# Two chained layers (transform convolution, selective scan): a new plan for the scan layer, its moments in PSUM, and table loads on change of set

## The chip, the cores and the metric

One NeuronCore of a Trainium2 chip runs one program. The time is device microseconds from launch to end, median of three runs, and apart from these runs there is one profiled execution, whose trace is read here. The engines are TensorE (PE in the profile; PEld is its weight load), VectorE (DVE), ScalarE (ACT), GpSimd (POOL) and SyncE (SP), which only issues DMAs. Each engine executes its own instructions in order and waits on semaphores.

## The reference

Layer 0 takes x of shape (4, 192, 128, 128) through a group norm, a 1x1 convolution to 48 channels, a fractional and a real Fourier branch, and a 1x1 convolution back, and adds x. Layer 1, which the change touches and the diff's title calls layer 2, does this with the result:

```python
x = x + _L1_conv_ref(_gn(x), ...)
# inside, with L = h * w tokens of 192 channels:
seq = (seq - mu) * lax.rsqrt(var + LN_EPS) * ln_g + ln_b
xs, z = jnp.split(jnp.einsum('blc,ec->ble', seq, in_proj_w), 2, axis=-1)
u = jax.nn.silu(conv1d(xs, conv_w, 4 taps, depthwise) + conv_b)
dt, Bm, Cm = jnp.split(jnp.einsum('bld,kd->blk', u, x_proj_w), ...)
dt = jax.nn.softplus(jnp.einsum('blr,dr->bld', dt, dt_proj_w) + dt_proj_b)
A = -jnp.exp(A_log)
# per token: 384 inner channels x 16 states
h = h * exp(dt * A) + (dt * u) * B_t
y = sum_over_states(h * C_t)
y = (y + u * Dp) * jax.nn.silu(z)
out = jnp.einsum('bld,cd->blc', y, out_proj_w)
```

## The kernel before

Layer 0 (`layer0`) takes the first 1.4 ms and is not touched. Layer 1 (`layer1`) cuts each of the 4 images into 32 **chunks** of T = 512 tokens, 128 chunks in all. The 384 inner channels are three tiles j = 0, 1, 2 of 128 partitions, and the 16 states are taken in pairs (G = 2). One tile with one pair is a **position**: 3 x 8 = 24 positions a chunk, 0 to 23, each with two scans. Below, "12.1" is the second scan of position 12.

**A scan.** `scans` (L938) runs `tensor_tensor_scan` on DVE over 512 tokens: h = da * h + db. The decay da = exp(dt * A) comes from ACT (`decay`, L860). The input db = dt * u * B comes in one of three ways, by the position's letter in `KINDS`: **V**, DVE multiplies (`product`, L881) into a PSUM bank; **O**, POOL multiplies both states at once (`inputs`, L892) into SBUF, and then da goes to a PSUM bank instead (`decay_there`); **P**, ACT scales the transposed dt * u (`scale`, L909, tile dbT, four buffers) and PE turns it back into PSUM (`turned_back`, L924). The PSUM tiles of these operands are called op and have three buffers, so an operand of scan s+3 has to wait until scan s is over. The da tiles in SBUF have four buffers.

**After the scans.** SP stores the last column of h as the next chunk's start (carry, L949). POOL multiplies h by C (hc, L951, 1,024 elements). Three positions later PE adds up hc over the states (`sums`, L964). The tile h has three buffers: position k+3 can start to write only when POOL has read h of position k and the carry DMA of k has landed.

**Around the scans.** Everything else that a chunk needs is placed by hand in `PLAN`: (position, phase, step, arguments). Positions below 0 are before the chunk's own first scan, those above 23 after its last, and the loop runs the plans of neighbouring chunks laid over each other; so a step at -20 falls on position 4 of the chunk being scanned, one at 32 on position 8 of a later one. A position's phases are S (before all else), A (after the first turning back and `sums`), M (between its two scans) and L (after them). The steps are, in order: `load_x`, `to_tokens` (PE), `moments` (DVE: bn_stats, bn_aggr), `rstd` (ACT, by Ln and Exp), `shift` (DVE), `normed` (ACT), `to_channels` (PE), `channels` (ACT, then a DMA that copies rows 0 to 63 of s, shifted by two tokens, to rows 64 to 127), `conv` (PE), `silu` (ACT), `proj_z` (PE), `proj_x` (PE), `xd_out` (ACT, then a DMA of B and C), `proj_dt` (PE), `softplus` (ACT), `dt_u` (POOL), `turn_b` and `b_out`, `turned` (PE) and `scale`, `dtu_copy` (ACT), `evacuate` (ACT), `turn` (PE), `gate` (DVE), `project_out` (PE), `add_x` (DVE). They share five PSUM banks, handed out in the order of release (`psum`, `done`).

**Queues.** SP issues the DMAs in the order of the code: the carry of each position, `load_x`, the DMA behind `xd_out`, the one behind `channels`, the output, and from position 19 on, through position 2 of the next chunk, the next chunk's B and C, copied to all partitions (`load_bc`, b and c, 512 KB each).

**Tables.** ACT's Silu, Softplus, and Ln with Exp lie in different table sets. `log_exp` (L661) loads the set for Ln and Exp; after each call of `silu` and of `softplus` the code calls it. The load of the Silu or Softplus set is added by the compiler in front of the first such instruction.

Of the kernel before, what the change touches and what calls it, by code (L numbers as in the profile page):

```python
# [121 lines left out]
def layer0(tc, x, xmid, st2, w):  # L122
# [409 lines left out]

KINDS = ("VOPPVVPO", "VOVPOVPP", "VOVPVPPO")

PLAN = (
# [21 lines left out]
)  # L559


def layer1(tc, xmid, out, st2, w, n_tok=S * S):
# [9 lines left out]
    with ExitStack() as ctx:  # L572
# [55 lines left out]
        ln = const("ln")  # L628
        wz = cp.tile([128, 2, NJ, 128], F32, name="wz")
        nc.sync.dma_start(out=wz, in_=w["wi"][:, :, 1])  # L630
        wc = cp.tile([128, NJ, 6, 128], F32, name="wc")
        for half in range(2):
            nc.sync.dma_start(
# [23 lines left out]
        NGR = NJ * NG  # L657
        got = [{} for _ in range(total)]

        def log_exp():  # L660
            nc.scalar.preload_act_table_set("natural_log_exp_and_others")  # L661

        def load_x(i):
            b, ch = divmod(i, NCHUNK)
# [19 lines left out]
        def row(g, blk):  # L684
            return g["X", blk // 2][0][:, blk % 2 * C : (blk % 2 + 1) * C]

        def moments(i, half):
            g = got[i]
            if half == 0:
                g["mv"] = tp.tile([128, NBLK, 2], F32, name="mv")  # L690
            st = tp.tile([128, 2, 6], F32, name="st")
            for blk in range(2):
                nc.vector.bn_stats(st[:, blk, :], row(g, 2 * half + blk))
            for blk in range(2):
                nc.vector.bn_aggr(g["mv"][:, 2 * half + blk, :], st[:, blk, :])

        def rstd(i):
            g = got[i]
            rs = g["rs"] = tp.tile([128, NBLK], F32, name="rs")
            nc.scalar.activation(rs, g["mv"][:, :, 1], AF.Ln, bias=eps)  # L700
            nc.scalar.activation(rs, rs, AF.Exp, scale=-0.5)  # L701

        def shift(i):
            g = got[i]
            sh = g["sh"] = tp.tile([128, NBLK], F32, name="sh")
            nc.vector.scalar_tensor_tensor(sh, g["mv"][:, :, 0], -1.0, g["rs"], ALU.mult, ALU.mult)

        def normed(i, half):
            g = got[i]
# [46 lines left out]
        def proj_z(i, j):  # L756
            g = got[i]
            psum(g, "z", j)
            z = g["z", j][0]
            nc.tensor.matmul(z, wz[:, 0, j, :], g["s"][:, 0, 3:], start=True, stop=False)  # L760
            nc.tensor.matmul(z, wz[0:64, 1, j, :], g["s"][0:64, 1, 3:], start=False, stop=True)  # L761

        def silu(i, us, zs):
            g = got[i]
            for j in us:
                t = g["u", j] = jp.tile([128, T], F32, name="u", bufs=5)
                nc.scalar.activation(t, g["c", j][0], AF.Silu, bias=cb[:, j : j + 1])  # L767
                done(g, "c", j)
            for j in zs:
                t = g["zs", j] = jp.tile([128, T], F32, name="zs", bufs=5)  # L770
                nc.scalar.activation(t, g["z", j][0], AF.Silu)
                done(g, "z", j)
            log_exp()

        def proj_x(i):
            g = got[i]
# [79 lines left out]
        def decay(s, da):  # L856
            n, k, q = states[s]
            j, sg = divmod(k, NG)
            st = sg * G + q
            nc.scalar.activation(da, got[n]["dt", j], AF.Exp, scale=A[:, j, st : st + 1])  # L860
            das[s] = da

# [31 lines left out]
        def turned(n, j):  # L894

            g = got[n]
            psum(g, "tu", j)
            g["pairs", j] = KINDS[j].count("P")
            for blk in range(NBLK):
                at = slice(blk * 128, (blk + 1) * 128)  # L900
                nc.tensor.transpose(g["tu", j][0][:, at], g["dtu", j][:, at], ident)  # L901

        def scale(n, j, sg):

            g = got[n]
            for st in range(sg * G, (sg + 1) * G):
                t = g["dbT", j, st] = scp.tile([128, NBLK, 128], F32, name="dbT")
                for blk in range(NBLK):
                    nc.scalar.activation(  # L909
                        t[:, blk, :], g["tu", j][0][:, blk * 128 : (blk + 1) * 128], AF.Identity,  # L910
                        scale=g["bT"][:, blk, st : st + 1],
                    )
            g["pairs", j] -= 1
            if not g["pairs", j]:
                done(g, "tu", j)
# [92 lines left out]
        def add_x(n, t):  # L1008
# [11 lines left out]
        does = dict(  # L1020
            load_x=load_x, to_tokens=to_tokens, moments=moments, rstd=rstd, shift=shift,
            normed=normed, to_channels=to_channels, channels=channels, conv=conv, proj_z=proj_z,
            silu=silu, proj_x=proj_x, xd_out=xd_out, proj_dt=proj_dt, softplus=softplus, dt_u=dt_u,
            turn_b=turn_b, b_out=b_out, dtu_copy=dtu_copy, turned=turned, scale=scale,
            evacuate=evacuate, turn=turn, gate=gate, project_out=project_out, add_x=add_x,
        )
# [193 lines left out]
```

## Time and profile before

| what | us |
|---|---|
| median of 3 runs (lowest, highest) | 11,274.59 (11,271.61, 11,287.38) |
| the profiled execution | 11,264.48 |
| its span, first to last instruction | 11,262.4 |
| PE, DVE, ACT, POOL busy in it | 10,025.0, 10,180.0, 9,562.4, 9,530.1 |
| mean granted TensorE clock | 0.958 |

The costliest groups of layer 1 on each engine are the scans on DVE (L938, two lines of 5,483.3 and 1,880.2 us), hc on POOL (L951, 7,220.3 us), the decays on ACT (L860, 3,191.1 and 1,096.8 us) and the transposing sums on PE (L964, 3,278.8 us). Reading such a table one has to keep in mind that these shares are of the whole span, layer 0 among them, where POOL does little. The times of the steps in layer 1 are read from the timeline of single chunks.

### The profile page before, as it was taken

The numbers are of one execution on the slowest core, as the hardware profiler recorded it, in microseconds if no ns is written. First come the engines' busy times: TensorE is split into PE (matmuls) and PEld (weight loads), VectorE is DVE, ScalarE is ACT, GpSimd is POOL, SyncE is SP. The second block draws the span as 40 slices with busy tenths as digits, with TensorE's granted clock in tenths as the row PEclk, the third lists the DMA queues.
The fourth block names the chain that finished last, engine by engine and source line by source line (L and its number), as shares of the span: only waits on it lengthen the run. The fifth ranks groups of instructions, "written<-read, shape, count | busy, mean of one in ns | idle before, by whom it ended". The sixth has DMA issues, their size and how long they took to land. (4 is left out here: it accounts for less than half of the span.)

```text
span 11262.4 us, 172048 instructions
## 1 busy us (share of the span) xinstructions
PE 10025.0 (89%) x56050; PEld 6906.9 (61%) x56050; DVE 10180.0 (90%) x11329; ACT 9562.4 (85%) x20200; POOL 9530.1 (85%) x4342
## 2 busy tenths in 40 slices
PE   4777789999999999999999999999999999999998
PEld 2434366666666666666666666666666666666666
DVE  5566589999999999999999999999999999999999
ACT  2323199999999999999999999999999999999998
POOL 0000089999999999999999999999999999999999
PEclk8888699999999999999999999999999999999999
DMA  8786733333333333333333333333333333333333
GB/s 234 190 219 174 206 115 108 105 117 106 107 117 105 108 117 106 107 117 107 106 117 107 106 117 111 102 117 110 103 117 111 102 117 112 101 117 113 100 117 91
DMA packets 1330368, 1366.53 MB, mean 121 GB/s; under 512 B 918345, under 2 KB 969790, under 8 KB 1328830
## 3 DMA queue, kind: packets, MB, share of 16 engines
q1 hardware_dynamic: 1308990, 1292.60, 40.0%
q0 software_dynamic: 13312, 50.34, 1.4%
q10 hardware_dynamic: 7168, 12.59, 0.3%
q8 instruction: 446, 7.31, 0.3%
q14 instruction: 452, 3.70, 0.1%
HBM read 1179.79 MB, written 155.33 MB: 119 GB/s over the span
## 5 line engine op out<-in xcount | busy, mean ns | idle before, releaser
L951 POOL TENSOR_TENSOR hc<-h,c 128x1024 f32<-128x1024 f32 x3072 | 7220.3, 2377 | 400.6 <-DVE h L938 371.5
L938 DVE TENSOR_TENSOR_SCAN h<-da,carry,op 128x512 f32<-128x512 f32 x4464 | 5483.3, 1262 | 150.5 <-ACT xd L784 69.2
L964 PE MATMUL ps<-ident,hc 128*128 128x128 f32 x24576 | 3278.8, 278 | 10.8 <-POOL hc L951 10.8
L860 ACT ACTIVATE da<-dt,c_A_log 128x512 f32<-128x512 f32 x4608 | 3191.1, 748 | 97.3 <-DVE h L938 93.1
L964 PEld LDWEIGHTS ps<-ident,hc 128*128 128x128 f32 x24576 | 2892.2, 144 | 485.1 <-issue 458.5
L909 ACT ACTIVATE dbT<-ps,bT 128x128 f32<-128x128 f32 x9216 | 2475.7, 402 | 76.4 <-PE ps L901 65.3
L754 PE MATMUL ps<-s,wc 128*128 128x512 f32 x4608 | 2162.5, 596 | 23.7 <-DMA s<-s 7.6
L938 DVE TENSOR_TENSOR_SCAN h<-op,carry,db 128x512 f32<-128x512 f32 x1488 | 1880.2, 1270 | 174.4 <-POOL db L892 103.1
L924 PE MATMUL op<-ident,dbT 128*128 128x128 f32 x9216 | 1462.7, 285 | 589.9 <-DVE h L938 581.2
L892 POOL TENSOR_TENSOR db<-dtu,b 128x1024 f32<-128x1024 f32 x768 | 1843.9, 2401 | 5.0 <-DMA b<-dbc 5.0
L924 PEld LDWEIGHTS op<-ident,dbT 128*128 128x128 f32 x9216 | 1091.7, 145 | 1031.9 <-ACT rs L701 396.5
L881 DVE TENSOR_TENSOR op<-ps,b 128x512 f32<-128x512 f32 x2304 | 1548.5, 672 | 9.4 <-ACT ps L842 9.4
L860 ACT ACTIVATE op<-dt,c_A_log 128x512 f32<-128x512 f32 x1536 | 1096.8, 714 | 392.9 <-DVE h L938 392.7
L754 PEld LDWEIGHTS ps<-s,wc 128*128 128x128 f32 x4608 | 795.4, 190 | 673.2 <-issue 628.5
L1003 PE MATMUL ps<-yg,c_woT 128*96 128x512 f32 x1536 | 710.5, 598 | 7.6 <-ACT u L767 0.3
L661 ACT ACT_TABLE_LOAD x513 | 658.2, 1283 | 9.8 <-PEq L1210 0.7
L808 POOL TENSOR_TENSOR dtu<-dt,u 128x512 f32<-128x512 f32 x384 | 486.0, 1281 | 53.8 <-ACT dt L801 53.8
L495 POOL DMA_DIRECT2D xmid<-xt x64 | 41.3, 645 | 566.9 <-DVE xt L491 526.5
L1003 PEld LDWEIGHTS ps<-yg,c_woT 128*96 128x96 f32 x1536 | 233.1, 163 | 384.9 <-issue 273.0
L761 PE MATMUL ps<-s,wz 64*128 64x512 f32 x768 | 431.0, 641 | 0.0
L760 PE MATMUL ps<-s,wz 128*128 128x512 f32 x768 | 419.3, 628 | 0.7 <-DVE xm L1010 0.5
L979 PE MATMUL ps<-ddp,u 128*128 128x128 f32 x3072 | 418.0, 280 | 0.0
(165 smaller groups left out, 9376.4 us busy)
## 6 DMA issues: line engine op xcount, KB each, us to landing
c<-dbc SPq DMA_DIRECT2D x1024, 512.0 KB, 5.9
b<-dbc SPq DMA_DIRECT2D x768, 512.0 KB, 5.1
xt<-in_x SPq DMA_DIRECT2D x176, 768.0 KB, 7.8
xmid<-xt POOLq DMA_DIRECT2D x64, 768.0 KB, 5.6
xm<-xmid SPq DMA_DIRECT2D x128, 384.0 KB, 3.4
carry<-h SPq DMA_DIRECT2D x3072, 1.0 KB, 1.9
out<-xm SPq DMA_DIRECT2D x128, 384.0 KB, 3.1
s<-s SPq DMA_DIRECT2D x128, 128.5 KB, 3.8
```

Source lines behind the costliest of these rows:

```text
L661: nc.scalar.preload_act_table_set("natural_log_exp_and_others")
L754: nc.tensor.matmul(g["c", j][0], wc[:, j, k, :], rhs, start=k == 0, stop=k == 5)
L808: nc.gpsimd.tensor_tensor(g["dtu", j], g["dt", j], g["u", j], ALU.mult)
L860: nc.scalar.activation(da, got[n]["dt", j], AF.Exp, scale=A[:, j, st : st + 1])
L881: nc.vector.tensor_tensor(dbs[s], g["dp", j][0], g["b", k % NG][:, q, :], ALU.mult)
L892: nc.gpsimd.tensor_tensor(db, _bc(g["dtu", j], 1, G), g["b", sg], ALU.mult)
L909: nc.scalar.activation(t[:, blk, :], g["tu", j][0][:, blk * 128 : (blk + 1) * 128], AF.Identity, scale=g["bT"][:, blk, st : st + 1],)
L924: nc.tensor.transpose(db[:, blk * 128 : (blk + 1) * 128], t[:, blk, :], ident)
L938: nc.vector.tensor_tensor_scan(h[:, q, :], das.pop(s), dbs.pop(s) if db is None else db[:, q, :], 0.0 if ch == 0 else g["before"][:, j, st ...
L951: nc.gpsimd.tensor_tensor(hc, h, g["c", "b", sg], ALU.mult)
L964: nc.tensor.matmul(py[:, blk, :], hc[:, q, blk * 128 : (blk + 1) * 128], ident, start=first, stop=sg == NG - 1 and q == G - 1 and blk == N ...
L1003: nc.tensor.matmul(g["po", t][0][0:CH], woT[:, j, t * CH : (t + 1) * CH], g["yg", j], start=j == 0, stop=j == NJ - 1,)
```

## The change

Five things are done, all in layer 1.

1. `KINDS` swaps two letters in the rows of j = 0 and j = 2, with the same number of each letter in a row as before.
2. `PLAN` is new as a whole. `silu` is split into `silu_u` and `silu_z`, one tile a call, and `scale` takes one state instead of a pair, so that these can be placed singly.
3. The mean and variance that `bn_aggr` yields go to eight spare columns (384 to 391) of the PSUM bank that holds the second half of the tokens, instead of the SBUF tile mv; `rstd` and `shift` read them there.
4. The second matmul of `proj_z` has all 128 rows instead of 64; the weights of the added rows are set to zero once.
5. `log_exp` remembers the set that is loaded, and is called in front of each decay and `rstd` instead of after `silu` and `softplus`.

```diff
-KINDS = ("VOPPVVPO", "VOVPOVPP", "VOVPVPPO")
+KINDS = ("VOPPVVOP", "VOVPOVPP", "VOVPPVOP")
 PLAN = (
-    (-36, "A", "load_x"), (-34, "L", "to_tokens", 0), (-32, "S", "moments", 0),
-    (-32, "A", "to_tokens", 1), (-31, "S", "moments", 1), (-31, "A", "rstd"), (-30, "S", "shift"),
-    (-30, "M", "normed", 0), (-30, "M", "normed", 1), (-29, "S", "to_channels", 0),
-    (-29, "A", "channels", 0), (-28, "M", "to_channels", 1), (-28, "M", "channels", 1),
-    (-27, "S", "conv", 0, 0), (-27, "L", "conv", 1, 0), (-26, "L", "conv", 1, 1),
-    (-25, "M", "conv", 0, 1), (-24, "M", "conv", 1, 2), (-22, "L", "conv", 2, 0),
-    (-21, "M", "conv", 0, 2), (-21, "L", "silu", (0, 1), ()), (-17, "S", "conv", 2, 1),
-    (-16, "A", "conv", 2, 2), (-15, "L", "proj_z", 0), (-15, "L", "silu", (2,), (0,)),
-    (-13, "M", "proj_x"), (-11, "S", "xd_out"), (-11, "M", "proj_dt"), (-10, "M", "softplus"),
-    (-9, "M", "turn_b"), (-8, "A", "b_out"), (-7, "A", "dt_u", 0), (-7, "A", "dt_u", 1),
-    (-3, "L", "turned", 0), (-3, "L", "scale", 0, 2), (-2, "S", "dtu_copy", 0),
-    (1, "S", "dt_u", 2), (1, "A", "scale", 0, 3), (2, "S", "scale", 0, 6),
-    (4, "M", "dtu_copy", 1), (6, "S", "turned", 1), (6, "A", "scale", 1, 3),
-    (10, "S", "scale", 1, 6), (10, "A", "scale", 1, 7), (10, "M", "evacuate", 0),
-    (10, "M", "proj_z", 2), (11, "A", "proj_z", 1), (11, "M", "silu", (), (1, 2)),
-    (11, "L", "turn", 0), (12, "L", "dtu_copy", 2), (13, "M", "gate", 0), (16, "L", "turned", 2),
-    (17, "S", "scale", 2, 3), (17, "L", "scale", 2, 5), (19, "S", "scale", 2, 6),
-    (19, "M", "evacuate", 1), (21, "A", "turn", 1), (22, "S", "gate", 1),
-    (26, "L", "evacuate", 2), (29, "A", "turn", 2), (30, "A", "gate", 2),
-    (31, "A", "project_out", 0), (32, "L", "add_x", 0), (34, "S", "project_out", 1),
-    (35, "M", "add_x", 1),
+    (-35, "M", "load_x"), (-34, "M", "to_tokens", 1), (-34, "L", "to_tokens", 0),
+    (-33, "L", "moments", 0), (-32, "A", "moments", 1), (-31, "L", "rstd"), (-30, "M", "shift"),
+    (-30, "M", "normed", 0), (-30, "M", "normed", 1), (-30, "M", "to_channels", 1),
+    (-29, "L", "to_channels", 0), (-29, "L", "channels", 0), (-27, "L", "channels", 1),
+    (-26, "S", "conv", 0, 0), (-26, "L", "conv", 1, 0), (-25, "L", "conv", 1, 1),
+    (-24, "L", "conv", 1, 2), (-22, "S", "conv", 0, 1), (-20, "S", "silu_u", 1),
+    (-20, "S", "conv", 0, 2), (-20, "S", "silu_u", 0), (-20, "M", "conv", 2, 0),
+    (-19, "M", "conv", 2, 1), (-17, "A", "conv", 2, 2), (-16, "L", "silu_u", 2),
+    (-15, "L", "proj_z", 0), (-15, "L", "silu_z", 0), (-13, "S", "proj_x"), (-13, "M", "xd_out"),
+    (-11, "M", "proj_dt"), (-10, "S", "softplus"), (-9, "M", "dt_u", 1), (-8, "S", "turn_b"),
+    (-8, "M", "dt_u", 0), (-8, "M", "b_out"), (-4, "A", "turned", 0), (-2, "M", "scale", 0, 6),
+    (-2, "L", "dtu_copy", 0), (-1, "A", "scale", 0, 4), (0, "A", "scale", 0, 5),
+    (0, "M", "scale", 0, 15), (1, "S", "scale", 0, 7), (2, "M", "scale", 0, 14),
+    (4, "S", "turned", 1), (7, "A", "dt_u", 2), (7, "A", "dtu_copy", 1), (7, "A", "scale", 1, 6),
+    (7, "M", "scale", 1, 7), (9, "M", "scale", 1, 15), (10, "S", "proj_z", 1),
+    (10, "A", "scale", 1, 14), (10, "L", "scale", 1, 13), (10, "L", "scale", 1, 12),
+    (10, "L", "evacuate", 0), (11, "S", "proj_z", 2), (11, "M", "silu_z", 1),
+    (11, "M", "silu_z", 2), (11, "L", "turn", 0), (13, "S", "gate", 0), (13, "A", "dtu_copy", 2),
+    (17, "S", "turned", 2), (17, "S", "scale", 2, 6), (17, "M", "scale", 2, 7),
+    (18, "M", "scale", 2, 8), (18, "M", "scale", 2, 9), (18, "M", "evacuate", 1),
+    (19, "L", "scale", 2, 15), (20, "S", "scale", 2, 14), (21, "A", "turn", 1),
+    (22, "S", "gate", 1), (27, "A", "evacuate", 2), (29, "S", "turn", 2), (29, "M", "gate", 2),
+    (32, "S", "project_out", 0), (32, "L", "add_x", 0), (34, "S", "project_out", 1),
+    (34, "L", "add_x", 1),
 )
...
+        nc.vector.memset(wz[64:128, 1], 0.0)
...
         def log_exp():
-            nc.scalar.preload_act_table_set("natural_log_exp_and_others")
+            if table[0] != "log_exp":
+                nc.scalar.preload_act_table_set("natural_log_exp_and_others")
+                table[0] = "log_exp"
...
+        def mean_var(g):
+            return g["X", 1][0][:, 2 * C : 2 * C + 2 * NBLK].rearrange("p (k m) -> p k m", m=2)
...
-                nc.vector.bn_aggr(g["mv"][:, 2 * half + blk, :], st[:, blk, :])
+                nc.vector.bn_aggr(mean_var(g)[:, 2 * half + blk, :], st[:, blk, :])
...
-            nc.scalar.activation(rs, g["mv"][:, :, 1], AF.Ln, bias=eps)
+            log_exp()
+            nc.scalar.activation(rs, mean_var(g)[:, :, 1], AF.Ln, bias=eps)
...
-            nc.vector.scalar_tensor_tensor(sh, g["mv"][:, :, 0], -1.0, g["rs"], ALU.mult, ALU.mult)
+            nc.vector.scalar_tensor_tensor(
+                sh, mean_var(g)[:, :, 0], -1.0, g["rs"], ALU.mult, ALU.mult
+            )
...
-            nc.tensor.matmul(z, wz[0:64, 1, j, :], g["s"][0:64, 1, 3:], start=False, stop=True)
+            nc.tensor.matmul(z, wz[:, 1, j, :], g["s"][:, 1, 3:], start=False, stop=True)
...
-        def silu(i, us, zs):
-            g = got[i]
-            for j in us:
-                t = g["u", j] = jp.tile([128, T], F32, name="u", bufs=5)
-                nc.scalar.activation(t, g["c", j][0], AF.Silu, bias=cb[:, j : j + 1])
-                done(g, "c", j)
-            for j in zs:
-                t = g["zs", j] = jp.tile([128, T], F32, name="zs", bufs=5)
-                nc.scalar.activation(t, g["z", j][0], AF.Silu)
-                done(g, "z", j)
-            log_exp()
+        def silu_u(i, j):
+            g = got[i]
+            t = g["u", j] = jp.tile([128, T], F32, name="u", bufs=5)
+            nc.scalar.activation(t, g["c", j][0], AF.Silu, bias=cb[:, j : j + 1])
+            table[0] = "silu"
+            done(g, "c", j)
+
+        def silu_z(i, j):
...
-            log_exp()
+            table[0] = "softplus"
...
             st = sg * G + q
+            log_exp()
             nc.scalar.activation(da, got[n]["dt", j], AF.Exp, scale=A[:, j, st : st + 1])
...
-        def scale(n, j, sg):
+        def scale(n, j, st):
...
-            for st in range(sg * G, (sg + 1) * G):
-                t = g["dbT", j, st] = scp.tile([128, NBLK, 128], F32, name="dbT")
-                for blk in range(NBLK):
...
+            t = g["dbT", j, st] = scp.tile([128, NBLK, 128], F32, name="dbT")
+            for blk in range(NBLK):
```

More of the change, by code (lines that the diff above doesn't have):

```diff
@@ L658, in layer1 @@
         got = [{} for _ in range(total)]
+        table = [None]
         def log_exp():
-            nc.scalar.preload_act_table_set("natural_log_exp_and_others")
+            if table[0] != "log_exp":
+                nc.scalar.preload_act_table_set("natural_log_exp_and_others")
+                table[0] = "log_exp"
         def load_x(i):
@@ L685, in row @@
             return g["X", blk // 2][0][:, blk % 2 * C : (blk % 2 + 1) * C]
+        def mean_var(g):
+            return g["X", 1][0][:, 2 * C : 2 * C + 2 * NBLK].rearrange("p (k m) -> p k m", m=2)
         def moments(i, half):
             g = got[i]
-            if half == 0:
-                g["mv"] = tp.tile([128, NBLK, 2], F32, name="mv")
             st = tp.tile([128, 2, 6], F32, name="st")
@@ L760, in proj_z @@
             nc.tensor.matmul(z, wz[:, 0, j, :], g["s"][:, 0, 3:], start=True, stop=False)
-            nc.tensor.matmul(z, wz[0:64, 1, j, :], g["s"][0:64, 1, 3:], start=False, stop=True)
-        def silu(i, us, zs):
+            nc.tensor.matmul(z, wz[:, 1, j, :], g["s"][:, 1, 3:], start=False, stop=True)
+        def silu_u(i, j):
             g = got[i]
-            for j in us:
-                t = g["u", j] = jp.tile([128, T], F32, name="u", bufs=5)
-                nc.scalar.activation(t, g["c", j][0], AF.Silu, bias=cb[:, j : j + 1])
-                done(g, "c", j)
-            for j in zs:
-                t = g["zs", j] = jp.tile([128, T], F32, name="zs", bufs=5)
-                nc.scalar.activation(t, g["z", j][0], AF.Silu)
-                done(g, "z", j)
-            log_exp()
+            t = g["u", j] = jp.tile([128, T], F32, name="u", bufs=5)
[4 more added lines that the diff above has]
+            g = got[i]
+            t = g["zs", j] = jp.tile([128, T], F32, name="zs", bufs=5)
+            nc.scalar.activation(t, g["z", j][0], AF.Silu)
+            table[0] = "silu"
+            done(g, "z", j)
         def proj_x(i):
@@ L897, in turned @@
             psum(g, "tu", j)
-            g["pairs", j] = KINDS[j].count("P")
+            g["pairs", j] = G * KINDS[j].count("P")
             for blk in range(NBLK):
@@ L901, in turned @@
                 nc.tensor.transpose(g["tu", j][0][:, at], g["dtu", j][:, at], ident)
-        def scale(n, j, sg):
+        def scale(n, j, st):
             g = got[n]
-            for st in range(sg * G, (sg + 1) * G):
-                t = g["dbT", j, st] = scp.tile([128, NBLK, 128], F32, name="dbT")
-                for blk in range(NBLK):
[L909 to L912, printed above, removed]
+            t = g["dbT", j, st] = scp.tile([128, NBLK, 128], F32, name="dbT")
+            for blk in range(NBLK):
+                at = slice(blk * 128, (blk + 1) * 128)
+                nc.scalar.activation(
+                    t[:, blk, :], g["tu", j][0][:, at], AF.Identity,
+                    scale=g["bT"][:, blk, st : st + 1],
+                )
             g["pairs", j] -= 1
@@ L1022, in layer1 @@
             normed=normed, to_channels=to_channels, channels=channels, conv=conv, proj_z=proj_z,
-            silu=silu, proj_x=proj_x, xd_out=xd_out, proj_dt=proj_dt, softplus=softplus, dt_u=dt_u,
+            silu_u=silu_u, silu_z=silu_z, proj_x=proj_x, xd_out=xd_out, proj_dt=proj_dt, softplus=softplus, dt_u=dt_u,
             turn_b=turn_b, b_out=b_out, dtu_copy=dtu_copy, turned=turned, scale=scale,
```

## The prediction

> **What bounds the kernel now.** First the table by stages, for layer 1 from its first scan to its last.
>
> ```profile
> 1425.00:11245.00 9820.00, 9056.32 (x52578) 6383.15 (x52577) 9315.27 (x10218) 9177.39 (x19665) 9423.24 (x4223) 0.98 0.37 109
> ```
>
> The columns are the stretch, PE, PEld, DVE, ACT, POOL, clock and DMA. Divided by 128: a chunk takes 76.7 us, in which POOL is busy 73.6, DVE 72.8, ACT 71.7, PE 70.8. No engine is the bound; 3.1 us a chunk is the most that a new order can gain while POOL's work stays. So the question is what DVE, which all others feed or follow, waits for. The view of waits, DVE alone, over 9,423 us or 122.8 chunks (us in total, times, longest):
>
> ```profile
> DVE yg L996 <- PE ps L989: 150.5, 122, 2.0
> DVE h L938 <- POOL db L892: 104.9, 151, 1.3
> DVE h L938 <- ACT xd L784: 70.4, 119, 1.2
> DVE h L938 <- PE op L924: 61.8, 138, 0.6
> DVE h L938 <- issue: 55.2, 43, 1.4
> DVE h L938 <- DMA carry<-h: 21.9, 40, 1.8
> ```
>
> Per chunk: 1.23 at a gate, 1.30 for "db" and "issue", 0.57 behind xd_out, 0.50 for a turned-back P, 0.18 for carries: 3.8 us. The second is partly misnamed, as the timelines of ACT and DVE around position 12 show:
>
> ```profile
> 6065.85 1.28 ACT L767 ACT_TABLE_LOAD   x1
> 6067.15 0.69 ACT L767 ACTIVATE u<-ps,c_cb 128x512 f32<-128x512 f32 x1
> 6067.87 0.60 ACT L771 ACTIVATE zs<-ps 128x512 f32<-128x512 f32 x1
> 6068.48 1.28 ACT L661 ACT_TABLE_LOAD   x1
> 6069.78 4.24 ACT L909 ACTIVATE dbT<-ps,bT 128x128 f32<-128x128 f32 x16
> 6073.80 0.70 ACT L973 COPY yt<-ps 128x512 f32<-128x512 f32 x1
> 6074.26 0.86 ACT L860 ACTIVATE da<-dt,c_A_log 128x512 f32<-128x512 f32 x1
> 6074.89 0.82 ACT L860 ACTIVATE op<-dt,c_A_log 128x512 f32<-128x512 f32 x1
> 6075.79 1.28 DVE L938 TENSOR_TENSOR_SCAN h<-op,carry,db 128x512 f32<-128x512 f32 x1 [1.35 <-issue]
> ```
>
> Scan 12.0 starts 0.08 after its decay ends at 6075.71: ACT had 9 us of other work in a row in front of it. The stall comes from where PLAN puts ACT's work.
>
> **The change, part by part.** I take durations as start to next start: a decay 0.62, a scaled state 1.00 (four in 4.02 above), a load 1.30 plus 0.1 for the tail of what runs before it, scan 1.19, product, gate, add_x 0.59.
>
> *Tables.* The Trainium skill ("ScalarE: Activation LUTs", "Rules for kernel authors") says to do all of one set before switching, and splitting silu into five calls speaks against that. But a load follows the order on ACT, not the calls. Position 4 holds silu_u 1 and 0; 8L has silu_u 2 and 9L silu_z 0, and between these no decay is issued, because 9 is an O position; 11M has both other silu_z; 14S has softplus. That is four switches away and four back: 8 loads, as now. Each cut would cost 2.6 us of ACT a chunk; none is added or removed in the steady state. The same page ("What ACT_TABLE_LOAD costs") gives 1.28 us and a drain of 1.38 for a switch; above, the load takes 1.28 and the next instruction starts 0.02 later. By the page 8 switches would cost 21.3 us, by the rows 11; I use the rows. Only in the prologue do three loads go (2.6 us of it on the way to the first scan).
>
> *Moments in PSUM.* bn_aggr (0.17) and Ln (0.33) keep their times, within 0.2 either way. shift is another matter:
>
> ```profile
> 6019.30 0.77 DVE L706 SCALAR_TENSOR_TENSOR sh<-mv,rs 128x4 f32<-128x4 f32 x1
> L706 DVE SCALAR_TENSOR_TENSOR sh<-mv,rs x128: 161/778/1075, 1383.6 to 11081.5; 128x4 f32<-128x4 f32 x128
> 6017.55 2.50 POOL L808 TENSOR_TENSOR dtu<-dt,u 128x512 f32<-128x512 f32 x2
> ```
>
> Four elements take 0.77 and the shift ends with POOL's instruction (6020.05); the minimum, 0.161, is the first shift, when POOL was idle. The skill ("GPSIMD Engine Reference", "1. Specifications") names it: POOL contends with DVE instructions that have two SBUF inputs. With the mean in PSUM only rs is left in SBUF: between 0.16 and 0.78, I take 0.2, so DVE's work falls from 72.8 to 72.2.
>
> *z projection.* 0.641 becomes 0.628 like its neighbour with 128 rows; the added rows were copied half a chunk earlier. Nothing: PE idles 6 us a chunk.
>
> *KINDS.* Equal letters, so equal work. An O in front of position 7 instead of behind it moves one db on POOL. There dt_u 2 also moves in front of db 9: hc 6, dt_u, db 9 are 2.32 + 1.23 + 2.35 = 5.9, and between the end of scan 6.1 and 9.0 DVE has 6.5. With POOL 0.6 behind, it just fits; I put 0.15 there (now 0.19 by those waits that are really db).
>
> *PLAN.* The new order has to be followed from engine to engine. Let 0 be the end of scan 8.1. ACT's last decay before its block, 11.1, waits for that scan (four da buffers). From there to dtu_copy 0 (22L), whose copy product 0.0 needs, ACT has 6 loads with tails (8.4), 27 decays (16.7), 11 scaled states (11.0), silu 2.3, xd_out 0.55, softplus 1.87, two dtu_copy 1.05, two evacuate 0.9, rstd 0.5, normed 1.6, channels 1.45, b_out 0.1: **46.4**. I find no wait of ACT inside: its operands from PE come earlier, the tightest being turned 2 by half a us. On the way:
> - op 12.0 is ready at 8.1, wanted at 9.5: today's 1.30 goes, because two of the scalings now follow it. op 12.1 comes at 11.9, wanted at 11.3: 0.6.
> - turn 0 waits for proj_x, and that for the PSUM bank which scale 1,12 frees at 10.8: 2.6 + 0.6 later gate 0 can start, at 14.1 instead of 13.6: 0.4.
> - xd_out ends at 15.0. Its DMA now stands in SP's queue at 11M, ahead of the carries of 11 and 12. Carry 11 lands at about 17.4, scan 14.0 would have its decay at 17.0: 0.4, in place of today's 0.57.
> - evacuate 1 moves one position forward, and neither conv nor a turning back stands in front of turn 1 any longer: gate 1's 1.23 goes.
> - 20.0 has its decay at 36.3 and its turned-back input (behind to_channels 1) at 36.5; DVE could be there at 36.0 at the earliest.
>
> - load_x goes from 12A to 13M, so its DMA is issued at about 16 and lands in 3.4; to_tokens, its reader, waits until 21.5 anyway, for banks that softplus frees. moments stand at 15L instead of 16S and lose 0.1 there. dt_u 1 and 0 come a position or two earlier on POOL, where its rests are; nothing.
>
> So product 0.0 starts at 46.5, and DVE, from 20.0 with 10.1 of work up to it, comes at the same time. Then come 19 scans (22.6), 8 products (4.7) and a gate (0.6) to the next 8.1: 27.9. Together 74.4: **ACT's block and DVE's stretch make one loop of 74.4 us**, above POOL's 73.6.
>
> In DVE's stretch lies a new wait. Carries land late while B and C are loaded (first line, 6029 to 6047 us) and soon otherwise (second, 6049 to 6072), and SP waits for ACT at two places:
>
> ```profile
> DMA to landing us min/median/max: 5.8/6.0/6.2
> DMA to landing us min/median/max: 1.8/1.8/2.1
> SPq L787 <- ACT xd L784: 406.3, 118, 3.6
> SPq L745 <- ACT s L739: 224.8, 117, 2.8
> ```
>
> The s copy moves from 20M to 21L, and ACT reaches channels 1 at about 45.3, the end of scan 22.1. Behind it in SP's queue stand two loads (1.1 to issue), then carry 22, issued 1.6 late. Scan 1.0 reuses that buffer 6.3 after 22.1. Landing between 1.8 and 6.2 after issue gives nothing to 1.5; two loads stand right in front, so I take 5.2: 0.5. With 0.15 at 9.0 and 0.15 for smaller carries the chunk is **75.2**.
>
> **Sum.** (76.7 - 75.2) x 128 = 192, and 2.6 in the prologue: 195 off the profiled execution's 11,264.5 (2.1 of that outside its span) gives 11,070. The median shown is 10.1 above the profiled execution, so I say **11,080**. Loop and carry uncertain by 0.8 a chunk either way, the forecast's own range is 10,980 to 11,185.
>
> **Rivals.** *POOL is the bound.* If ACT's tails overlap more and the carries land in time, DVE never starves and POOL's 73.6 stays, with 0.2 of rests: 2.9 x 128 = 371, 10,900. For it: POOL's load by position is smoother, and its rests now (3.1) are almost all waits for DVE. Against: ACT would have to save 0.6 in its block, where no wait is left to save.
>
> *The stalls only move.* Period 76.5 to 76.9, 11,275: four small waits above are estimates of 0.4 to 0.6, and each could be today's size. Against: the two largest of today have no successor at their place.
>
> *Slower, by SP's queue.* If ACT reaches channels 1 one us later than I reckon, carry 22 is issued 2.6 late; landing 6.2 later it holds scan 1.0 for 2.5, and this falls into the loop: 74.4 + 2.5 + 0.3 = 77.2, + 0.5 x 128 = 11,340. It decides from about 2.0 us at scan 1.0 on; for it speaks that SP is in order and the loads saturate the DMA for 25 us of each chunk, against it that SP's own backlog is then smaller, because the loads are also later.
>
> *The change doesn't do what it says* for the tables: no load is saved in the steady state, which is already in the sum.
>
> **Chances.** A measurement here can tell 0.2% (22 us) from no change. Forecast 0.60, POOL as bound 0.15, moved stalls 0.09 (nearly all within 0.2%), slower 0.16. Hence faster 0.76, same 0.08, slower 0.16. The range 10,940 to 11,290 leaves out most of the slower case and half of POOL's.
>
> **What would show it.** Right: about 75.2 us a chunk, 8 loads in it, shift near 0.2, gate 1 without a wait, ACT busy without a break from scan 8.1 to dtu_copy 0, and waits at 12.1, gate 0 and 14.0 of about half a us each. Wrong: a wait for carries over 1 us at 1.0 or 14.0, ACT idle inside its block, more than 8 loads, or POOL idle less than 1 us.

## The result, and the profile after

The changed kernel takes 11,177.49 us (median of 4 runs, 11,165.33 to 11,188.61), the kernel before 11,276.4 beside it. The ratio is 0.9911, with a 95% interval of 0.9894 to 0.9928: 99 us, or 0.9%, faster. The forecast was 11,080.

The profiled execution has a span of 11,186.7 us, 75.7 less than before. Cut at four events of the trace:

| part of the span, us | before | after |
|---|---|---|
| layer 0, whose code is the same | 1,355.0 | 1,368.8 |
| from there to the first scan of layer 1 (prologue) | 70.2 | 76.8 |
| first scan to the end of the last | 9,820.0 | 9,725.7 |
| the rest | 17.2 | 15.4 |

Layer 0 ends anywhere between 1,353 and 1,372 us in the profiles of this study, so the scans' row, 94 us less, is the one to compare. The table by stages of after has for that row (stretch, PE, PEld, DVE, ACT, POOL, clock, DMA):

```profile
1445.60:11171.30 9725.70, 8961.77 (x52588) 6378.93 (x52586) 9294.51 (x10217) 9161.56 (x19665) 9408.66 (x4223) 0.98 0.37 110
```

That is 76.0 us a chunk, and DVE's work is 72.6 as against 72.8: shift became shorter, but the moments steps longer (below). The gain is mostly in waits. The view of waits of after, DVE alone, same stretch (us in total, times, longest):

```profile
DVE h L953 <- ACT op L875: 126.6, 128, 1.4
DVE h L953 <- DMA carry<-h: 109.8, 149, 1.9
DVE h L953 <- PE op L939: 90.5, 153, 7.3
DVE h L953 <- POOL hc L966: 34.0, 89, 1.4
DVE h L953 <- ACT da L875: 28.0, 94, 1.9
DVE yg L1011 <- PE ps L1004: 7.8, 9, 1.8
```

Over the scans of before, gate 1's wait was 155.2 and is now 7.8, and the waits named db, issue and xd are all but gone (4.4, 1.1 and none). In their place stand one in front of scan 11.0 (first line, 0.99 a chunk) and the carries, which went from 23.0 to 109.8. Three steps can be seen at work in the timelines of one chunk, DVE first:

```profile
6049.24 2.49 DVE L953 TENSOR_TENSOR_SCAN h<-da,carry,op 128x512 f32<-128x512 f32 x2 [0.99 <-ACT op L875]
...
6064.99 0.62 DVE L702 BATCH_NORM_STATS2 st<-ps 128x6 f32<-128x192 f32 x2
6065.53 0.40 DVE L704 BATCH_NORM_AGGREGATE ps<-st 128x2 f32<-128x6 f32 x2
6065.97 0.63 DVE L702 BATCH_NORM_STATS2 st<-ps 128x6 f32<-128x192 f32 x2
6066.63 0.42 DVE L704 BATCH_NORM_AGGREGATE ps<-st 128x2 f32<-128x6 f32 x2
...
6074.05 0.14 DVE L716 SCALAR_TENSOR_TENSOR sh<-ps,rs 128x4 f32<-128x4 f32 x1
```

Shift takes 0.14 instead of 0.77. The two moments steps now take 1.97 from start to the next scan (6064.99 to 6066.96): bn_stats of the second half reads the bank that bn_aggr of the first writes to, and starts 0.04 after that has ended (6065.93). With the results in SBUF it starts before the end (the lines of e7 below). And PE shows what really stands in front of scan 11.0:

```profile
6046.72 1.02 PE L772 MATMUL ps<-s,wz 128*128 128x512 f32 x2
6047.58 1.02 PE L773 MATMUL ps<-s,wz 128*128 128x512 f32 x2
6048.44 0.60 PE L939 MATMUL op<-ident,dbT 128*128 128x128 f32 x4
```

The turning back that scan 11.0 reads ends 0.2 before it, and it stands behind the four matmuls of proj_z 1, which take 1.72 us. "ACT op" on DVE's line is a name inferred wrongly, as "issue" was before: e2 and e14 below show that PE is meant.

For the experiments, each chunk is cut in two, as the forecast did: the block, from the end of scan 8.1 to the start of product 0.0, and the stretch from there to the next 8.1. The times are means over 123 chunks of each trace, and so are the waits of single scans below. Each ratio is to runs of the kernel before made beside that kernel.

| kernel | block | stretch | chunk | ratio to before, 95% interval | median us |
|---|---|---|---|---|---|
| before | 48.66 | 28.08 | 76.74 | 1 | |
| forecast for after | 46.5 | 28.7 | 75.2 | | 11,080 |
| after | 47.11 | 28.87 | 75.97 | 0.9911 (0.9894 to 0.9928) | 11,177.49 |
| e1_s_copy_late | 47.13 | 28.95 | 76.08 | 0.9925 (0.9911 to 0.9938) | 11,189.42 |
| e2_z_after_turn | 47.13 | 28.90 | 76.03 | 0.9918 (0.9906 to 0.9930) | 11,180.86 |
| e3_moments_sbuf | 47.79 | 28.87 | 76.66 | 0.9983 (0.9976 to 0.9989) | 11,262.74 |
| e4_switch_in_block | 49.90 | 28.88 | 78.77 | 1.0232 (1.0218 to 1.0246) | 11,536.04 |
| e5_loads_in_rest | 47.22 | 30.35 | 77.58 | 1.0082 (1.0068 to 1.0096) | 11,372.51 |
| e7_rs_psum | 46.94 | 28.96 | 75.90 | 0.9902 (0.9888 to 0.9915) | 11,169.26 |
| e8_load_after_carry | 47.15 | 29.55 | 76.71 | 0.9992 (0.9984 to 1.0000) | 11,272.17 |
| e10_before_rs_psum | 48.04 | 28.37 | 76.40 | 0.9956 (0.9942 to 0.9970) | 11,227.83 |
| e11_h4_hc4 | 47.00 | 28.09 | 75.09 | 0.9813 (0.9800 to 0.9827) | 11,070.44 |
| e12_h4_rs | 46.98 | 28.11 | 75.09 | 0.9807 (0.9794 to 0.9821) | 11,062.27 |
| e13_before_h4 | 48.70 | 27.81 | 76.51 | 0.9974 (0.9965 to 0.9983) | 11,237.29 |
| e14_scale_early | 46.91 | 28.18 | 75.09 | 0.9823 (0.9809 to 0.9836) | 11,069.96 |

### The profile page after: what moved, and what is told of

It reads as the page before. It is cut to its first block, busy times and chain, and to the rows that moved or that the text cites. A ratio compares the mean times of both kernels' runs of the same rounds, so it can differ in the third digit from the quotient of the medians.

```text
span 11186.7 us, 171424 instructions
## 1 busy us (share of the span) xinstructions
PE 9950.4 (89%) x56050; PEld 6911.8 (62%) x56050; DVE 10160.0 (91%) x11330; ACT 9542.3 (85%) x20197; POOL 9513.5 (85%) x4342
## 5 line engine op out<-in xcount | busy, mean ns | idle before, releaser
L924 ACT ACTIVATE dbT<-ps,bT 128x128 f32<-128x128 f32 x9216 | 2583.6, 396 | 12.6 <-PE op L939 11.7
L953 DVE TENSOR_TENSOR_SCAN h<-op,carry,db 128x512 f32<-128x512 f32 x1488 | 1853.4, 1267 | 98.0 <-DMA carry<-h 81.7
L939 PE MATMUL op<-ident,dbT 128*128 128x128 f32 x9216 | 1422.6, 281 | 242.8 <-ACT dbT L924 168.8
L916 PE MATMUL ps<-ident,dtu 128*128 128x128 f32 x1536 | 262.4, 297 | 337.0 <-ACT bT L834 337.0
L916 PEld LDWEIGHTS ps<-ident,dtu 128*128 128x128 f32 x1536 | 179.2, 148 | 393.2 <-ACT bT L834 366.8
L202 DVE BATCH_NORM_STATS2 st<-xt 96x6 f32<-96x512 f32 x512 | 322.2, 677 | 101.7 <-DMA xt<-in_x 100.5
```

Of the source, the lines that this page charges most:

```text
L924: nc.scalar.activation(t[:, blk, :], g["tu", j][0][:, at], AF.Identity, scale=g["bT"][:, blk, st : st + 1],)
L939: nc.tensor.transpose(db[:, blk * 128 : (blk + 1) * 128], t[:, blk, :], ident)
L953: nc.vector.tensor_tensor_scan(h[:, q, :], das.pop(s), dbs.pop(s) if db is None else db[:, q, :], 0.0 if ch == 0 else g["before"][:, j, st ...
```

## Experiments

"Loop theory" below is the forecast's: a chunk lasts as long as ACT's block and DVE's stretch together, and what lies beside them costs nothing. The rivals are that every microsecond of an engine counts, or that waits are only replaced.

### Moments in PSUM: what is a 4-element instruction worth?

**e3_moments_sbuf** undoes the moments part alone.

```diff
         def mean_var(g):
-            return g["X", 1][0][:, 2 * C : 2 * C + 2 * NBLK].rearrange("p (k m) -> p k m", m=2)
+            return g["mv"]
...
+            if half == 0:
+                g["mv"] = tp.tile([128, NBLK, 2], F32, name="mv")
```

> Mean and variance go to SBUF again (tile mv, as in the kernel before), all else as changed. Loop theory: the two moments steps take 1.52 instead of 1.97 us, scan 16.0 starts 0.45 earlier, ACT's wait for it at decay 17.1 (0.44 a chunk, inside the block) goes, and the longer shift (0.78 instead of 0.14) lies in front of 20.0, where DVE waits anyway: 0.3 to 0.45 us a chunk less, about 11,125. Rival, DVE's work counts: 0.19 us more a chunk, 11,200.

Measured: 85 us slower than after, beyond what either theory gave. The row of shift among the groups of its tile (min/median/max in ns):

```profile
L718 DVE SCALAR_TENSOR_TENSOR sh<-mv,rs x128: 163/1701/2284, 1388.4 to 11084.3; 128x4 f32<-128x4 f32 x128
```

And, in the timelines of POOL and DVE, one shift beside POOL's work:

```profile
6020.90 4.66 POOL L968 TENSOR_TENSOR hc<-h,c 128x1024 f32<-128x1024 f32 x2
...
6023.89 1.69 DVE L718 SCALAR_TENSOR_TENSOR sh<-mv,rs 128x4 f32<-128x4 f32 x1
```

Shift is not 0.77 here but 1.70, and ends at 6025.58, 0.02 after POOL's (6025.56). Over all chunks its end lies 0.02 (median) from the end of a POOL instruction. So it is not slowed by a factor: it waits until POOL's running instruction is over, and how long that is depends on where in POOL's 2.3 us the new order puts it. The block grows by 0.68.

**e10_before_rs_psum** does the converse: the kernel before, in its old order, where shift gets its rs from PSUM.

```diff
+            rp = g["rp"] = g["X", 1][0][:, 2 * C + 2 * NBLK : 2 * C + 3 * NBLK]
+            nc.scalar.activation(rp, rs, AF.Exp, scale=-0.5)
...
-            nc.vector.scalar_tensor_tensor(sh, g["mv"][:, :, 0], -1.0, g["rs"], ALU.mult, ALU.mult)
+            nc.vector.scalar_tensor_tensor(sh, g["mv"][:, :, 0], -1.0, g["rp"], ALU.mult, ALU.mult)
```

> The kernel before, with a second, tiny Exp that writes the reciprocal deviation into a PSUM bank where shift reads it: the moments part of the change alone (shift with one SBUF input) in the old order. If every microsecond of VectorE counts: shift falls from 0.78 to 0.14 us, so 82 us less: about 11,197 us. If shift's time lies ahead of the wait of gate 1 and only lengthens that wait: no change, 11,279 us. In between if the second Exp delays the block by its 0.1 to 0.2 us.

Measured: 52 us less, between the two. The row of shift:

```profile
L708 DVE SCALAR_TENSOR_TENSOR sh<-mv,ps x128: 147/151/158, 1383.5 to 11041.4; 128x4 f32<-128x4 f32 x128
```

Its maximum is 0.158, with the mean still in SBUF: moving one of the two inputs out of SBUF is enough to be free of POOL. The block falls by 0.62, all of shift's 0.63; longer waits at scans 1.0 and 3.0, most of them for carries, take 0.29 back in the stretch. So of the change's 99 us about half is to be had by this alone, and the rest of the change without it (e3) is 0.9983 of before, some 19 us. They make 71 of the 99; in the new order the part is worth more, 85, because shift would wait 1.70 there. The rest (KINDS, PLAN, z projection and tables) was not taken apart; its 19 us are one sum.

**e7_rs_psum** puts the same into after: mean and variance back in SBUF, the second Exp into the bank, so that bn_aggr no longer writes where the next bn_stats reads.

```diff
-            return g["X", 1][0][:, 2 * C : 2 * C + 2 * NBLK].rearrange("p (k m) -> p k m", m=2)
+            return g["mv"]
...
+            rp = g["rp"] = g["X", 1][0][:, 2 * C + 2 * NBLK : 2 * C + 3 * NBLK]
+            nc.scalar.activation(rp, rs, AF.Exp, scale=-0.5)
...
-                sh, mean_var(g)[:, :, 0], -1.0, g["rs"], ALU.mult, ALU.mult
+                sh, mean_var(g)[:, :, 0], -1.0, g["rp"], ALU.mult, ALU.mult
```

> The kernel after, with the moments' mean and variance in an SBUF tile again, and a second, tiny Exp that writes the reciprocal deviation into the PSUM bank too, where shift reads it: so shift keeps one SBUF input, and bn_aggr no longer writes into the bank that the next bn_stats reads. Theory (the moments steps' growth from 1.52 to 1.97 us is what put the wait of 0.44 us before op 17.1 into ScalarE's block): shift stays at 0.14 us, the two moments steps take about 1.5 us, op 17.1's wait falls by about 0.4 us, the second Exp adds 0.1 to 0.2 us to the block, so 0.3 us a chunk less: about 11,135 us. Rival (that wait is scan 16.0's own order and stays): 11,177 to 11,200 us.

Measured: 8 us less than after, within the intervals of both. The moments steps in DVE's timeline:

```profile
6042.79 0.62 DVE L704 BATCH_NORM_STATS2 st<-ps 128x6 f32<-128x192 f32 x2
6043.33 0.30 DVE L706 BATCH_NORM_AGGREGATE mv<-st 128x2 f32<-128x6 f32 x2
6043.54 0.60 DVE L704 BATCH_NORM_STATS2 st<-ps 128x6 f32<-128x192 f32 x2
6044.05 0.30 DVE L706 BATCH_NORM_AGGREGATE mv<-st 128x2 f32<-128x6 f32 x2
6044.28 2.45 DVE L957 TENSOR_TENSOR_SCAN h<-da,carry,op 128x512 f32<-128x512 f32 x2
```

They take 1.49 instead of 1.97, and ACT's wait of 0.44 in front of op 17.1 is gone, as the theory said. The second Exp takes part of this back, as ACT's timeline shows:

```profile
6049.94 0.18 ACT L714 ACTIVATE ps<-rs 128x4 f32<-128x4 f32 x1
```

At the end ACT is 0.30 earlier with dtu_copy 0, but the block falls by only 0.17, because DVE is now the later of the two: scan 20.0 waits 0.61 instead of 0.44, gate 1 0.16 instead of 0.05, and product 0.0 starts 0.23 after the copy that it reads (0.09 in after). The cost was real and hid in part beside another path (on which the granted clock bears: see the section on the prediction).

### Table loads: does a microsecond of ACT count, and where?

**e4_switch_in_block** puts a switch back where the change avoids it, behind silu_u 2.

```diff
             done(g, "c", j)
+            if j == 2:
+                log_exp()
```

> silu_u 2 at 8L is followed at once by the load of the set for Ln and Exp, so that silu_z 0 at 9L needs another load: two loads more a chunk, 2.6 us, inside ACT's block. Loop theory: all of it is paid, 2.6 x 128 = 333 us more, about 11,510. Rival, ACT has 4.4 us of rest a chunk and POOL 2.5, which take most of it: under 100 us more, below 11,280.

Measured: 10 loads a chunk instead of 8, and 359 us more. The two that were added, in ACT's timeline of one chunk:

```profile
6041.53 1.28 ACT L668 ACT_TABLE_LOAD   x1
...
6043.98 1.28 ACT L787 ACT_TABLE_LOAD   x1
```

The block takes all of it, 2.79 us, or 1.40 a load, which is the forecast's 1.30 and a tail of 0.1; the stretch stays. **e5_loads_in_rest** puts two loads at 2L, where ACT rests for 1.44 us.

```diff
+        def extra(i):
+            nc.scalar.preload_act_table_set("silu_and_others")
+            table[0] = "silu"
+            log_exp()
...
-    (22, "S", "gate", 1), (27, "A", "evacuate", 2), (29, "S", "turn", 2), (29, "M", "gate", 2),
+    (22, "S", "gate", 1), (26, "L", "extra"), (27, "A", "evacuate", 2), (29, "S", "turn", 2), (29, "M", "gate", 2),
```

> The kernel after, with two more table loads in each chunk (silu's set and back to exp's), put at position 2L, where the trace of after shows ScalarE resting (1.44 us of idle time at position 3). The loop theory (a microsecond of ScalarE counts only inside its block, from the end of scan 8.1 to product 0.0): 0 to 0.4 us a chunk, so 11,177 to 11,230 us. The rival theory (each microsecond of ScalarE counts, wherever it lies): the two loads cost what the two loads inside the block cost, 2.79 us a chunk, so about 11,530 us.

Measured: 195 us more, between the two. The block is nearly untouched, as the loop theory has it, but the stretch grows by 1.48. Its view of waits, DVE alone, over 2,000 to 11,000 us (118 chunks):

```profile
DVE yg L1016 <- PE ps L1009: 161.3, 121, 1.7
```

And ACT's timeline around position 3 of one chunk:

```profile
6021.65 1.28 ACT L672 ACT_TABLE_LOAD   x1
6022.94 1.28 ACT L668 ACT_TABLE_LOAD   x1
6024.23 0.59 ACT L993 COPY yt<-ps 128x512 f32<-128x512 f32 x1
```

Evacuate 2 stands behind the loads, turn 2 behind that, and gate 2, which had no wait in after, waits 1.34 us in the middle of DVE's stretch. The loads take 2.57, the rest took up 1.08 of it (1.44 fell to 0.36), and 1.48 came out. A rest absorbs its own length, no more, when a chain to the bound engine hangs on what follows it; the loop theory's "nothing outside the block" was too generous.

### The carries

**e1_s_copy_late** issues the copy of s behind carry 22 (22L).

```diff
-    (-26, "S", "conv", 0, 0), (-26, "L", "conv", 1, 0), (-25, "L", "conv", 1, 1),
+    (-26, "S", "conv", 0, 0), (-26, "L", "copy_s"), (-26, "L", "conv", 1, 0), (-25, "L", "conv", 1, 1),
```

> The DMA that copies s is issued one step later, at 22L instead of 21L, so that SP no longer stands in front of carry 22 and its two loads until ACT has done channels 1. Loop theory (ACT's block and DVE's stretch from product 0.0 to scan 8.1 make one loop, and the wait of scan 1.0 for carry 22, 0.78 us a chunk in the changed kernel, lies in it): the wait falls to about 0.15, the chunk from 75.98 to 75.35 us, the time from 11,177 to about 11,100. Rival, the DMA rings are full anyway: carry 22 lands as late as before, 11,177. Rival, POOL takes the wait over: less than 0.2 us a chunk gained, above 11,150.

Measured: no gain. Scan 1.0's wait went from 0.78 to 0.04, but scan 3.0's from 0.12 to 0.78. Its view of waits, same window:

```profile
DVE h L955 <- PE op L941: 160.3, 255, 2.3
...
DVE h L955 <- DMA carry<-h: 20.0, 31, 1.2
```

Conv reads the copied s, now late (PE waits 54.0 us in front of it for that copy, in the same window), and on PE the turning back of 3.0 stands behind it. **e8_load_after_carry** leaves s alone and moves the load of pair 2 behind carry 22:

```diff
-                    load_bc(n + 1, k - (NGR - BCL))
+                    sg = k - (NGR - BCL)
+                    for late in {2: (), 3: (2, 3)}.get(sg, (sg,)):
+                        load_bc(n + 1, late)
```

> The kernel after, with the load of B and C of the next chunk's pair 2 issued one position later, behind the carry of scan 22 on SyncE's queue instead of ahead of it. Theory (scan 1.0's wait of 0.78 us is for a carry that is stuck in the queue, and the time ahead of scan 8.1 is VectorE's): the wait falls to about 0.15 us, VectorE's stretch falls from 28.87 to about 28.25 us, so about 80 us less: 11,097 us. Rival (the wait goes to the next one, as it did when the copy of s was issued later: B and C of pair 2 late, or TensorE): 11,177 us.

Measured: 95 us slower than after, worse than both. Same view and window:

```profile
DVE h L953 <- DMA carry<-h: 144.3, 174, 2.6
```

Carry 22 lands 2.2 us after its scan (6.6 in after, both medians) and 1.0 no longer waits; but four loads now stand in front of carry 23, which lands 1.2 later than in after, and scan 2.0 waits 1.16. The queue only hands the delay on.

**e11_h4_hc4** takes away what makes a scan wait for a carry at all: the buffer of h. A fourth h is paid for by the fifth hc.

```diff
-            h = scp.tile([128, G, T], F32, name="h", bufs=3)
+            h = scp.tile([128, G, T], F32, name="h", bufs=4)
...
-            hc = scp.tile([128, G, T], F32, name="hc", bufs=5)
+            hc = scp.tile([128, G, T], F32, name="hc", bufs=4)
```

> The kernel after, with four buffers for h instead of three and four for hc instead of five (the same room in all). A scan that waits for a carry waits because the buffer of h that it writes is the one that the carry's transfer still reads, three positions back. Loop theory: scan 1.0's 0.74 us on carry and hc go, VectorE's stretch falls from 28.87 to 28.15 us, and the 0.36 us at 14.0 and 20.0 lie beside ScalarE's block, so about 90 us less: 11,085 us. Rival (the wait is only replaced, as when the copy of s or the load was moved: by TensorE's turned_back 3.0, or by GpSimd for want of a fifth hc): 11,177 us or more.

Measured: 11,070.44, or 107 us less than after; the stretch falls by 0.78, the block by 0.11. The view of waits of this kernel over its scans:

```profile
DVE h L953 <- ACT op L875: 125.0, 127, 1.3
DVE h L953 <- PE op L939: 111.4, 261, 8.1
DVE h L953 <- POOL hc L966: 30.1, 100, 0.3
DVE h L953 <- ACT da L875: 24.4, 123, 0.4
```

No carry is left among them, though each still lands as late as before. **e13_before_h4** is the same edit in the kernel before.

> The kernel before, with four buffers for h and four for hc: the same edit in the old order. Theory (the long waits for carries are made by the new order, which puts the copy of s in front of carry 22): the old order has only 0.2 us a chunk of them at 1.0 to 4.0, so 0 to 28 us less: 11,255 to 11,284 us. Rival (the buffers would have helped the old order as much, and say nothing on the change): 107 us less, 11,177 us.

Measured: 11,237.29, beside 11,267.78 for the kernel before in those runs: 30 us less, just over the upper end of the theory's 28, and far from the rival's 107. So three buffers of h instead of four cost the old order 30 us and the new one 107 (with a fifth hc given up in both): the change gave some 77 us of its gain back here.

### Two paths in the block

**e2_z_after_turn** takes proj_z 1 from in front of turning back 11.0.

```diff
-    (7, "M", "scale", 1, 7), (9, "M", "scale", 1, 15), (10, "S", "proj_z", 1),
+    (7, "M", "scale", 1, 7), (9, "M", "scale", 1, 15), (10, "M", "proj_z", 1),
```

> proj_z 1 goes from 10S to 10M, behind the turning back of 11.0 and 11.1, which it held up on PE. Loop theory: the wait of scan 11.0 (0.99 us a chunk) stands beside ACT's block and not in the loop; it goes, waits for ACT at 12.1, gate 0 or 14.0 take its place, and the time stays within 0.2% of 11,177. Rival, the DVE waits add up: 0.99 x 128 = 127 us less, 11,050.

Measured: no difference to be told from after. Scan 11.0's 0.99 went, and 12.0, 12.1 and gate 0, which had no wait, took 0.17, 0.34 and 0.39; 14.0 keeps its 0.35. Two lines of the view of waits, 2,000 to 11,000 us; they stand at 5.9 and 119.3 in after. The first now holds the wait of gate 0, the second that of 12.1 alone:

```profile
DVE yg L1011 <- PE ps L1004: 54.6, 130, 1.0
DVE h L953 <- ACT op L875: 39.7, 112, 0.6
```

**e12_h4_rs** joins e11 and e7:

> The four buffers of h and of hc, with the moments in SBUF and the reciprocal deviation in the PSUM bank as well, both in one kernel. Loop theory: the stretch falls by 0.7 us and the block by the 0.17 us that the second took off it alone, so 110 us less than after: about 11,065 us. Rival (waits are only replaced): 11,170 us.

Measured: 11,062.27, the fastest here, within the interval of e11. Its granted clock over the scans was lower, 0.957, than in e11 (0.972) and in after (0.977); blocks are longer where the clock is not full (see the next section), so what the second edit is worth beside the first is not settled. **e14_scale_early** takes one scaled state out of ACT's block of e12.

```diff
-    (7, "M", "scale", 1, 7), (9, "M", "scale", 1, 15), (10, "S", "proj_z", 1),
+    (7, "M", "scale", 1, 7), (7, "M", "scale", 1, 15), (10, "S", "proj_z", 1),
```

> The kernel with four buffers of h and hc and both forms of the moments, and with one scaled state (scale 1, 15) at 7M instead of 9M: from inside ScalarE's block to just ahead of it, where ScalarE rests for 1.29 us at positions 7 and 8. Loop theory: the rest takes it, the block falls by the 1.0 us of a scaled state and the stretch stays, so 1.0 us a chunk less, if no other wait comes up: 10,935 us; a part of it, 10,935 to 11,010, if GpSimd with its 73.5 us a chunk or TensorE is late next. Rival (each microsecond of ScalarE counts, or the block isn't what binds): no change, 11,062 us.

Measured: no gain, as the rival said. The views of waits of e12 and of e14, 2,000 to 11,000 us:

```profile
DVE h L957 <- PE op L943: 153.7, 242, 1.2
DVE h L957 <- ACT op L879: 116.2, 119, 1.3
```

```profile
DVE h L957 <- PE op L943: 272.6, 361, 1.4
```

ACT starts 0.88 earlier into the decays behind its first two table loads (medians, from the end of 8.1: 5.80 instead of 6.68), so scan 11.0 could have started earlier, but it waits 0.98 as before, now under PE's name: turning back 11.0 stands behind proj_z 1. From there DVE is late, and ACT's lead is given back in waits for dbT and op buffers: 0.35 is left in front of silu_z 1, 0.13 at op 17.1. So e2 freed PE and was held by ACT, e14 freed ACT and was held by PE: the first third of the block has two paths of nearly one length. Both edits in one kernel were not tried, so that they gain together is only argued.

## Why the prediction was right in direction and twice too large

**Right.** Two waits of before (1.23 at gate 1, 1.30 under "db" and "issue") do go, and the 0.4 put at 14.0 came as 0.34. Two more loads inside the block are paid in full (e4), at 1.4 each, and not at what the drain of 1.38 that the forecast quotes would make of it (2.66). Loads stay at 8; shift falls to 0.14; POOL, at 73.5 us a chunk, is not the bound. "The stalls only move" is half of what happened: over the scans, DVE's waits went from 3.9 us a chunk to 3.2.

**Where it was wrong.** Of the forecast's 1.5 us a chunk 0.77 came: the block is 0.6 over the forecast and the stretch 0.17.

- "I find no wait of ACT inside", 46.4. The sum was right, the statement was not. ACT waits 0.45 in front of op 17.1 and 0.14 in front of evacuate 1, and dtu_copy 0 ends at 47.0; without these waits it would end at 46.4. One chunk of after, from ACT's timeline:

```profile
6068.28 0.69 ACT L875 ACTIVATE op<-dt,c_A_log 128x512 f32<-128x512 f32 x1 [0.42 <-DVE h L953]
...
6075.34 0.58 ACT L988 COPY yt<-ps 128x512 f32<-128x512 f32 x1 [0.48 <-PE ps L979]
```

  The first wait hangs on a term called free: "bn_aggr (0.17) and Ln (0.33) keep their times, within 0.2 either way". The moments steps grew by 0.45. e7 takes that away, and ACT is 0.47 earlier at op 17.1. That its block keeps 0.44 of the 0.6 has a first cause in the second Exp (0.18). The rest goes with TensorE's granted clock, for which the forecast has no term: in these traces it drops to half for short stretches. Where it was full through the whole block (43 of 123 in e7), the block is 46.62, which is the forecast and the Exp; in the other 80 it is 47.11, and scan 20.0, whose turned-back input stands behind normed and to_channels 1, starts at 36.77 instead of 36.56. In after the two are 46.82 (45 blocks) and 47.26, with the wait at evacuate 1 in the latter alone; in before 48.53 and 48.72. No run changes the clock, so that it makes the difference is argued from these traces.
- Shift. The forecast took it off DVE's work ("from 72.8 to 72.2") and gave it no term in the loop of 74.4. It is the largest part: 52 us in the old order (e10), where ACT's rest inside the block falls from 0.90 to 0.30 with it, because normed needs what shift writes; and 85 in the new one (e3), where its price would have been 1.70 and not the 0.78 of the old trace. The new order without it is worth some 19 us. So the direction was right in good part by luck: by a term that the loop did not count on.
- Carry 22, "I take 5.2: 0.5". It was issued 1.4 late and landed 5.1 later, much as forecast (1.6 and 5.2). But DVE reaches scan 1.0 5.9 after the end of 22.1, not 6.3: four scans and two products, by the forecast's own durations. So scan 1.0 waited 0.78. The mechanism was right, the size 0.3 short; the 0.15 put at 9.0 came as nothing and the 0.15 for smaller carries as about that. What I missed is larger than the term: the forecast priced this wait and took it as given, where a buffer, not the queue, was the thing that e11 shows to be worth 107 us.
- The waits at 12.1 (0.6) and gate 0 (0.4) came as 0.99 at 11.0, because proj_z 1, whose four matmuls take 1.72 on PE in front of turning back 11.0, has no term in the forecast. That the two sizes agree is luck; without this hold-up 12.1 and gate 0 wait 0.34 and 0.39 (e2).
- The prologue: "three loads go". They do (9 to 6), but it grew from 70.2 to 76.8 us. The Ln that rstd begins with starts 29.2 us after layer 0 instead of 26.8, since both halves of the tokens now stand in front of the first bn_stats and Ln's own load behind the second; the other 4.2 us come later, and which step makes them is not shown.

In the profiled execution the missing 0.77 a chunk are 98 us and the prologue 9; layer 0's scatter put 14 on top, and the rest of the span took 2 off. The median lies 11 below that execution (11,188.61), where the forecast had reckoned with 10 above. That leaves the 97 by which the forecast was too low. So the last 21 us are luck too: with the median 10 above, the time would have been about 11,199, outside the forecast's own range of 10,980 to 11,185.

## What to carry over

In a loop of several engines, one engine's sum can be right and still too short, because it waits for what it hands to the others (op 17.1). Look for the second path of the same length, because an edit that frees one of them gained nothing here (e2, e14). When a wait names a DMA, ask first which buffer it guards: shifting the DMA in its queue only moved the wait (e1, e8), one more buffer removed it (e11). And price the instruction that seems too small to matter: four elements on DVE, kept off a second SBUF input, gave half of this change.

## What the hardware did that I had not expected

With two SBUF inputs, shift did not run at a slower rate beside POOL; it ended with POOL's instruction. It took 0.163 when POOL was idle (the minimum in e3), 0.78 (median) in the old order and 1.70 in the new one, its end 0.02 (median) from an end on POOL in both, and 0.13 to 0.16 in every chunk as soon as one of its inputs lay in PSUM. The Trainium skill ("GPSIMD Engine Reference", "1. Specifications") has the contention; the length of the wait comes from these runs.

The second is the moments steps: with bn_aggr's results in the bank that the next bn_stats reads, they took 1.97 instead of 1.49. In the trace of after, the second bn_stats step and the later bn_aggr wait for a semaphore that DVE's own instructions raise, and start 0.03 after the one before them has ended; in e7 they start about 0.08 before. So the time goes into an order between uses of one tile; that PSUM as a place is slow here is not shown.
